# A two-layer macaron transformer in float32: the ternary weights' rounding cut into sixteenths, halves of the next group normalized a tile later, and the last 64 hidden features multiplied in rounded float32

## The chip, the cores and the metric

The kernel runs on one core of one Trainium2 chip. The metric is the device time of one execution in microseconds; lower is better. The time before is 2608.78 us, the median of 3 runs (2608.46 to 2609.09). Five engines work beside each other, each with its own queue in program order: TensorE (PE; its weight loads are PEld), VectorE (DVE), ScalarE (ACT), GpSimd (POOL) and SyncE (SP), whose queue issues nearly all DMAs here.

## The reference, cut to what matters

The input is 8 x 1024 tokens of 256 features, float32. Six blocks follow each other; each works on a layer norm of `x` and adds to `x`.

```python
x = x + 0.5 * L0_ffn(layernorm(x), w_gate, w_up, w_down)   # fp4 stage 1
x = x + L0_attn(layernorm(x), ...)                         # decaying linear attention
x = x + 0.5 * L0_ffn(layernorm(x), w_gate, w_up, w_down)   # fp4 stage 2, the same weights
x = x + 0.5 * L1_ffn(layernorm(x), W1, b1, W2, b2)         # ternary weights, gelu
x = x + L1_attn(layernorm(x), ...)                         # linear attention with memories
x = x + 0.5 * L1_ffn(layernorm(x), W1, b1, W2, b2)

def L0_ffn(x, w_gate, w_up, w_down):        # 256 -> 704 -> 256
    h = silu(fp4(x) @ fp4(w_gate).T) * (fp4(x) @ fp4(w_up).T)
    return fp4(h) @ fp4(w_down).T           # fp4: blocks of 16 share a scale max|.|/6,
                                            # each value goes to the nearest of 0, .5, 1, 1.5, 2, 3, 4, 6
def ternary(w):                             # W1 and W2, 256 x 1024 each
    return clip(round(w / mean(abs(w))), -1, 1)
```

## The kernel before, in words

The 8192 tokens are 64 tiles of 128 (`i`, `NT` = 64), four tiles to a group (`g`, `NG` = 16). `x` stays in SBUF throughout. The diff touches the two fp4 stages (`ffn_fp4`, L745), the preparation that the first of them carries along, and the decaying attention at one place.

**One tile of an fp4 stage** is one turn of the loop at L994. PE makes gate and up products in halves of 352 columns (`products`, L831: `pg` and `pu`, 2 contraction parts each; the trace has two records for each float32 matmul). ACT makes silu of `pg` (L846), DVE multiplies by `pu` (L848): that is `h`, 704 wide. Then `h` is rounded to the fp4 grid: DVE makes the blocks' scales (`scale`, L783 to L787), POOL multiplies `h` by their reciprocals (L791), ACT makes magnitudes (L795), and DVE rounds in two steps (L858, the second into `gd`, bfloat16, 768 wide with 64 columns of zeros). `gd` is turned by a DMA transpose (`gt`, L884). The scales are turned on PE (L863), sent to DRAM and read back, spread over partitions, as `ht` (L871 and L876). Two tiles later POOL multiplies `ht` by `gt` (`scaled_turn`, L905, at L899). One turn after that, `down` (L925) makes six products of 128 features each (the last has 64 features and 64 zeros) into `po`, and DVE adds `po` to `x` (L941).

**Halves of the next group.** The layer norm of group `t` is prepared during the tiles before it, in halves of two tiles: ACT normalizes (L317 and L325) at turns 4t-7 and 4t-5, DVE makes scales (L783 to L787 on `xn`) at the even turns 4t-6 and 4t-4, and DVE rounds (L858 on `xn`) at the odd turns 4t-5 and 4t-3. POOL multiplies `xn` (L791) after the scales, and `xt` by the turned grid (L899, `xt<-gtx,xt`) two turns after the rounding. The statistics for it (L235, L236, L248 to L264) are shares of work that `PLANS` (L346) lays over the turns, each group with a due turn; `ln.advance` does the shares of a turn.

**Order.** `pin` (L190) ties each instruction to the one emitted before it on the same engine, so that in these stages each queue runs in the order of the text. On DVE a turn is: L848 of the first half, the two L858 of the tile before, L848 of the second half, the scales of `h`, the work on `xn`, a share of statistics, L941, and last what `prepared(i)` (L946) brings.

**`prepared`** runs in the first fp4 stage only. At turns 7 and 27 it loads W1 and W2 (raw_w, 2048 columns per partition), and at every fourth turn after that it does one of four steps (`prep_ternary`, L674): the sum of magnitudes (L683), the total, and two roundings of 1024 columns each, three DVE instructions long (L699, L700, L703). At turn 44 it calls `prep_memory` (L719), which makes constants for the second attention, mostly on POOL.

**The end of a stage.** The last two tiles are turned by PE transposes (`turn`, L911) and not by DMA.

Of the kernel before, what the change touches and what calls it, by code (L numbers as in the profile page):

```python
# [18 lines left out]
P = 128  # L19
# [20 lines left out]
def macaron_kernel(  # L40
# [227 lines left out]
    def statistics(sizes, dues):  # L268
# [78 lines left out]
        "start": ((2, 1, 1, 2, 4, 4, 2), [max(0, G * (g - 2) + 1) for g in range(NG)]),  # L347
        "fp4": ((2, 1, 1, 2, 4, 4, 2), [max(0, G * (g - 2) + 1) for g in range(NG)]),
# [95 lines left out]
    wd = w_f0.tile([P, NC, D], F32, name="wd")  # L444
    nc.gpsimd.memset(wd[DCH[-1][1] :, NC - 1, :], 0.0)
# [190 lines left out]
    def prep_down_turn(ps, tag):  # L636
        for i, (k0, kn) in enumerate(DCH):
            pt = ps.tile([P, D], F32, tag=tag, name="ptd")
            for c in range(2):
                pin(  # L640
                    nc.tensor.transpose(
                        pt[:kn, c * P : (c + 1) * P], wd_n[:, c, k0 : k0 + kn], ident
                    )
                )
            pin(nc.scalar.copy(wd[:kn, i, :], pt[:kn, :]))
# [28 lines left out]
    def prep_ternary(w, raw_w, prep, ps, tag):  # L674

        n0 = w.shape[1]
        n = n0 * w.shape[2]
        ab = prep.tile([P, 1], F32, tag="t_ab", name="t_ab")
        rc = prep.tile([P, 1], F32, tag="t_rc", name="t_rc")

        def sums():
            pin(
                nc.vector.tensor_reduce(  # L683
                    ab, raw_w.rearrange("p k n -> p (k n)"), AX.X, ALU.add,
                    apply_absolute_value=True,
                )
            )

        def total():
            pa = ps.tile([P, 1], F32, tag=tag, name="pa")  # L690
            pin(nc.tensor.matmul(pa, lhsT=ones, rhs=ab, start=True, stop=True))
            pin(nc.vector.tensor_scalar(rc, pa, 1.0 / (P * n), 1e-8, ALU.mult, ALU.max))
            pin(nc.vector.reciprocal(rc, rc))

        def rounded(q):
            part = slice(q * n0 // 2, (q + 1) * n0 // 2)
            wf = raw_w[:, part, :].rearrange("p k n -> p (k n)")
            lo = prep.tile([P, n // 2], F32, tag="t_lo", name="t_lo")
            pin(nc.vector.tensor_scalar(wf, wf, rc, None, ALU.mult))  # L699
            pin(nc.vector.tensor_scalar(lo, wf, -0.5, None, ALU.is_lt))  # L700

            pin(
                nc.vector.scalar_tensor_tensor(  # L703
                    w[:, part, :].rearrange("p k n -> p (k n)"), wf, 0.5, lo,
                    ALU.is_gt, ALU.subtract,
                )
            )

        return sums, total, lambda: rounded(0), lambda: rounded(1)
# [35 lines left out]
    def ffn_fp4(prepare, after):  # L745
        with ExitStack() as st:
# [13 lines left out]
            nc.gpsimd.memset(gd[:, NI:], 0.0)  # L760
# [18 lines left out]
            def scale(v, pool, at, mul=nc.gpsimd, sc=None):  # L779
                vb = v.rearrange("p (b k) -> p b k", k=16)  # L780
                _, nb, _ = vb.shape
                am, sp = qp[:, at : at + nb], qp[:, at + nb : at + 2 * nb]
                pin(nc.vector.tensor_reduce(am, vb, AX.X, ALU.max, apply_absolute_value=True))  # L783
                pin(nc.vector.tensor_scalar(sp, am, -1.0 / 6.0, -1e-12, ALU.mult, ALU.min))
                rs = pool.tile([P, nb], F32, tag="q_rs", name="q_rs")
                pin(nc.vector.tensor_scalar(rs, sp, -FP4_TIE, None, ALU.mult))
                pin(nc.vector.reciprocal(rs, rs))  # L787
                if sc is None:
                    sc = pool.tile([P, nb], F32, tag="q_sc", name="q_sc")
                copies.append(lambda: pin(nc.scalar.copy(sc, sp)))  # L790
                pin(mul.tensor_tensor(vb, vb, rs[:, :, None].to_broadcast([P, nb, 16]), ALU.mult))  # L791
                return sc
# [111 lines left out]

            def scaled_turn(i):  # L905
                hs.pop(i)
                ht = spreading.pop(i)
                multiplied(ht, turning.pop(i))
                hts[i] = (ht, P)

            def turn(i):  # L911
                h, _ = hs.pop(i)
                ht = hp.tile([P, NC, P], F32, tag="ht", name="ht", bufs=HT_BUFS)
                for c0, c1 in ((0, 4), (4, 5), (5, 6)):
                    kn = DCH[c0][1]
                    pa = ps_t.tile([P, 4, P], F32, tag="pt", name="pt")
                    for c in range(c0, c1):
                        k0 = DCH[c][0]
                        pin(
                            nc.tensor.transpose(pa[:kn, c - c0, :], h[:, k0 : k0 + kn], ident)  # L920
                        )
                    pin(nc.scalar.copy(ht[:kn, c0:c1, :], pa[:kn, : c1 - c0, :]))
                hts[i] = (ht, DCH[-1][1])

            def down(i, ps=ps_o, tag="po"):  # L925
                g, j = divmod(i, G)
                ht, tail = hts.pop(i)
                po = ps.tile([P, D], F32, tag=tag, name="po")
                for c in range(NC):
                    kn = tail if c == NC - 1 else P  # L930
                    pin(
                        nc.tensor.matmul(  # L932
                            po,
                            lhsT=ht[:kn, c, :],
                            rhs=wd[:kn, c, :],
                            start=(c == 0),
                            stop=(c == NC - 1),
# [8 lines left out]
            def prepared(i):  # L946
# [10 lines left out]
                for k, i0 in enumerate((7, 27)):  # L957
# [8 lines left out]
                    if i0 < i <= i0 + 16 and i % G == i0 % G:  # L966
                        raw_w[1][(i - i0) // G - 1]()
                    if i == i0 + 16:
                        raw_w_stack.close()
                if i == 44:  # L970
                    with behind():
                        prep_memory()
# [14 lines left out]

            xn = None
# [5 lines left out]
            for i in range(NT + 3):  # L994
                g, j = divmod(i, G)
                h = hp.tile([P, NI], F32, tag="h", name="h") if i < NT else None

                to = (i + 7) // G
                to_do = to < NG and i > 0
                half = 0 if j in (1, 2, 3) else 1  # L1000
# [3 lines left out]
                pts = None  # L1004
                for q in range(2):
# [18 lines left out]
                    if 0 < i < NT and q == 0:  # L1024
                        magnitudes(hs[i - 1][0], qp[:, 0:NI])
                        if by_dma(i - 1):
                            round_grid(hs[i - 1][0], qp[:, 0:NI], gd[:, :NI])
                    if i == NT - 1:
# [15 lines left out]
                for to_, half_ in list(xgrids):  # L1044
                    gx, at = xgrids[to_, half_]
                    if at == i - 1:
                        gt = lnp.tile([P, G, P], BF16, tag="gtx", name="gtx", bufs=1)
                        pin(nc.sync.dma_start_transpose(out=gt, in_=gx))
                        xgrids[to_, half_] = (gt, at)
# [7 lines left out]
                if to_do and j % 2 == 1:  # L1057
                    if j == 1:
                        to_n, tiles = to, (0, 1)
                        if xn is None:  # L1060
                            xn = xn_pool.tile([P, G, D], F32, tag="xn", name="xn")
                    else:
                        to_n, tiles = (i + 5) // G, (2, 3)
                    if to_n < NG:
                        for n in tiles:
                            ln.normalize(xn, to_n, n, pin)
                if by_dma(i - 3):
                    scaled_turn(i - 3)
                if NT - 2 <= i - 2 < NT:
                    turn(i - 2)  # L1070
                for key in list(xgrids):
                    gt, at = xgrids[key]
                    if at == i - 2:
                        xgrids.pop(key)
                        to_m, half_m = key
                        multiplied(xts[to_m][:, G * half_m : G * half_m + G, :], gt)
                if i < NT:
                    own = scales[i % 2] if by_dma(i) else None
                    if own is not None:
                        scale(h, hp, NI, sc=own[:, : NI // 16])  # L1080
# [4 lines left out]
                    if j % 2 == 0 and i > 1:  # L1085
                        to_s, half_s = ((i + 6) // G, 0) if j == 2 else ((i + 4) // G, 1)
                        if 1 < to_s < NG:
                            scale(
                                x_part(half_s), lnp, NI + 88,
                                sc=own[:, NC * 8 : NC * 8 + 2 * D // 16],  # L1090
                            )
                            xhalf[i] = (to_s, half_s)
                    if j % 2 == 1 and i > 1:
                        to_r, half_r = ((i + 5) // G, 0) if j == 3 else ((i + 3) // G, 1)
                        if 1 < to_r < NG:
                            v = x_part(half_r)
                            mg = ps_t.tile([P, 2 * D], F32, tag="pt", name="mgx")
                            magnitudes(v, mg)
                            gx = v.bitcast(BF16)[:, 0 : 2 * D]
                            round_grid(v, mg, gx)  # L1100
                            xgrids[to_r, half_r] = (gx, i)
# [10 lines left out]
                if prepare and i == DOWN:  # L1112
                    prep_down_turn(ps_t, "pt")
# [240 lines left out]
    def attn_decay(after):  # L1354
        with ExitStack() as st:
# [101 lines left out]
            for i in range(n + 3):  # L1457
# [56 lines left out]
                if i < n:  # L1514
# [5 lines left out]
                    ln.advance(i)  # L1520
                if n - 16 <= i < n - 4:
# [563 lines left out]
```

## Time and profile before

| what | us |
|---|---|
| median of 3 runs | 2608.78 |
| the profiled execution | 2604.35 |
| its span, first to last instruction | 2602.6 |
| PE busy in the span | 2504.2 (96%) |
| DVE busy | 2107.9 (81%) |
| ACT busy | 1235.8 (47%) |
| POOL busy | 902.6 (35%) |
| first gate product of tile 8 and of tile 63, fp4 stage 1 | 114.6 and 537.5 |
| first gate product of tile 18 and of tile 63, fp4 stage 2 | 1144.4 and 1479.1 |

A row of the timeline gives the start in us, the duration in us, the engine, the line, the operation, the tiles written and read with their sizes, the count, and in brackets the idle time before it with what ended it. Instructions of one kind that follow each other are merged in one row. In DVE rows, durations of neighbours overlap by about 0.1 us, so costs are read from start to start.

### The profile page before, as it was taken

The numbers are of one execution on the slowest core, as the hardware profiler recorded it, in microseconds if no ns is written. First come the engines' busy times: TensorE is split into PE (matmuls) and PEld (weight loads), VectorE is DVE, ScalarE is ACT, GpSimd is POOL, SyncE is SP. The second block draws the span as 40 slices with busy tenths as digits, with TensorE's granted clock in tenths as the row PEclk, the third lists the DMA queues.
The fourth block names the chain that finished last, engine by engine and source line by source line (L and its number), as shares of the span: only waits on it lengthen the run. The fifth ranks groups of instructions, "written<-read, shape, count | busy, mean of one in ns | idle before, by whom it ended". The sixth has DMA issues, their size and how long they took to land.

```text
span 2602.6 us, 52695 instructions
## 1 busy us (share of the span) xinstructions
PE 2504.2 (96%) x20426; PEld 1864.2 (72%) x20426; DVE 2107.9 (81%) x5040; ACT 1235.8 (47%) x2785; POOL 902.6 (35%) x895
## 2 busy tenths in 40 slices
PE   4899999999999998999999999999999999999999
PEld 2566776766666665677777789995677767678998
DVE  7899999858777678998889789657888888879864
ACT  5344444433433333444444366665555555437664
POOL 4555555521100102555555400004555555540000
PEclk9899999999999999999999999999999999999999
DMA  7455565510000001556555300000000000000001
GB/s 218 99 111 120 119 114 112 110 32 2 2 2 2 2 2 29 113 117 116 115 114 118 81 1 1 1 1 1 2 2 2 2 2 2 2 2 25 33 33 42
DMA packets 197883, 130.32 MB, mean 50 GB/s; under 512 B 137824, under 2 KB 173696, under 8 KB 197632
## 3 DMA queue, kind: packets, MB, share of 16 engines
q1 hardware_dynamic: 196688, 125.75, 22.3%
q8 instruction: 161, 2.64, 0.4%
q0 software_dynamic: 240, 0.54, 0.1%
q14 instruction: 90, 0.74, 0.1%
q10 hardware_dynamic: 704, 0.66, 0.1%
HBM read 78.67 MB, written 16.52 MB: 37 GB/s over the span
## 4 chain that ended last, share of the span: by engine, by line
PE 80%; DVE 11%; ACT 3%; DMA 3%; issue 2%; POOL 1%; SPq 1%; DVEq 0%; POOLq 0%; ACTq 0%
PE po L932 10%; PE po L1207 9%; PE pg L835 9%; PE ph L1180 9%; PE pu L835 8%; PE sc L1250 5%; PE py L1334 5%; PE pq L1348 4%; PE pkv L1348 4%; PE pk L1348 4%; PE po L1348 4%; PE py L1316 2%; PE pmo L1765 2%; DVE at L1259 1%; DMA gtx<-xn 1%
## 5 line engine op out<-in xcount | busy, mean ns | idle before, releaser
L835 PE MATMUL pg<-wgu,xt 128*128 128x352 f32 x1024 | 350.0, 465 | 13.4 <-ACT sg L846 13.1
L932 PE MATMUL po<-wd,ht 128*128 128x256 f32 x1536 | 356.0, 382 | 2.3 <-DVE x L941 1.8
L835 PE MATMUL pu<-wgu,xt 128*128 128x352 f32 x1024 | 348.9, 464 | 2.1 <-DVE h L848 1.9
L932 PEld LDWEIGHTS po<-wd,ht 128*128 128x128 f32 x1536 | 291.7, 191 | 66.0 <-issue 4.1
L791 POOL TENSOR_TENSOR h<-h,q_rs 128x704 f32<-128x704 f32 (+1 forms) x128 | 176.3, 1378 | 419.9 <-DVE q_rs L787 419.9
L846 ACT ACTIVATE sg<-pg 128x352 f32<-128x352 f32 x256 | 117.8, 460 | 399.3 <-PE pg L835 394.0
L835 PEld LDWEIGHTS pg<-wgu,xt 128*128 128x128 f32 x1024 | 194.9, 192 | 108.5 <-ACT sg L846 21.1
L835 PEld LDWEIGHTS pu<-wgu,xt 128*128 128x128 f32 x1024 | 187.1, 193 | 103.3 <-issue 14.7
L1207 PE MATMUL po<-w,hl 128*128 128x256 f32 x1024 | 243.9, 280 | 1.4 <-DVE hl L1191 1.2
L1207 PE MATMUL po<-w,hh 128*128 128x256 f32 x1024 | 243.4, 280 | 0.0
L1881 POOL TENSOR_TENSOR mo<-mo 128x256 f32<-128x256 f32 x192 | 164.3, 856 | 195.0 <-DVE mo L1778 186.5
L899 POOL TENSOR_TENSOR ht<-gt,ht 128x768 f32<-128x768 bf16 x124 | 206.4, 1664 | 0.0
L1180 PE MATMUL ph<-xh,w 128*128 128x512 f32 x512 | 204.4, 401 | 1.4 <-ACT hf L1188 0.6
L1180 PE MATMUL ph<-xl,w 128*128 128x512 f32 x512 | 202.2, 396 | 0.0
L1191 DVE TENSOR_TENSOR hl<-hf,hh 128x512 fp32r<-128x512 f32 x256 | 168.2, 683 | 39.6 <-ACT hh L1189 36.1
L1207 PEld LDWEIGHTS po<-w,hl 128*128 128x128 f32 x1024 | 192.1, 188 | 4.5 <-DVE hl L1191 2.5
L1207 PEld LDWEIGHTS po<-w,hh 128*128 128x128 f32 x1024 | 192.0, 188 | 2.6 <-DVE x L1215 0.3
L848 DVE TENSOR_TENSOR h<-sg,pu 128x352 f32<-128x352 f32 x256 | 131.6, 514 | 60.0 <-PE pu L835 53.1
L1188 ACT ACTIVATE hf<-ph,b1c 128x512 f32<-128x512 f32 x256 | 168.3, 696 | 18.5 <-PE ph L1180 16.1
L1259 DVE TENSOR_TENSOR at<-sc,dec 128x512 f32<-128x512 f32 x256 | 158.5, 681 | 16.6 <-PE sc L1250 16.5
L1259 DVE TENSOR_TENSOR at<-sc,tri 128x512 f32<-128x512 f32 x256 | 164.6, 678 | 0.4 <-PE sc L1250 0.4
L1189 ACT CAST hh<-hf 128x512 fp32r<-128x512 f32 x256 | 149.2, 628 | 17.0 <-PE po L1207 15.2
(276 smaller groups left out, 5304.0 us busy)
## 6 DMA issues: line engine op xcount, KB each, us to landing
ht<-sd SPq DMA_DIRECT2D x124, 384.0 KB
xt<-sd SPq DMA_DIRECT2D x56, 256.0 KB
sd<-sct SPq DMA_DIRECT2D x124, 64.0 KB
x<-in_x SPq DMA_DIRECT2D x15, 512.0 KB
out<-x SPq DMA_DIRECT2D x15, 512.0 KB
raw_w<-in_w_t SPq DMA_DIRECT2D x2, 1024.0 KB
gt<-gd SPq DMA_TRANSPOSE x124
gtx<-xn SPq DMA_TRANSPOSE x56
```

Source lines behind the costliest of these rows:

```text
L791: pin(mul.tensor_tensor(vb, vb, rs[:, :, None].to_broadcast([P, nb, 16]), ALU.mult))
L835: nc.tensor.matmul(ps, lhsT=xts[g][:, 2 * j + k, :], rhs=wgu[:, k, (2 * q + of_up) * NHALF : (2 * q + of_up + 1) * NHALF], start=(k == 0), ...
L899: nc.gpsimd.tensor_tensor(wide.rearrange("p c t -> p (c t)"), grid.rearrange("p c t -> p (c t)"), wide.rearrange("p c t -> p (c t)"), ALU. ...
L932: nc.tensor.matmul(po, lhsT=ht[:kn, c, :], rhs=wd[:kn, c, :], start=(c == 0), stop=(c == NC - 1),)
L1180: nc.tensor.matmul(ph, lhsT=w1[:, k, f * P : (f + 1) * P], rhs=xt[:, k, :], start=(k == 0 and xt is xh), stop=(k == 1 and xt is xl),)
L1188: nc.scalar.activation(hf, ph, AF.Gelu, bias=b1c[:, f : f + 1])
L1189: nc.scalar.copy(hh[:, f, :], hf)
L1191: nc.vector.tensor_tensor(hl[:, f, :], hf, hh[:, f, :].bitcast(F32), ALU.subtract)
L1207: nc.tensor.matmul(po, lhsT=ht[:, f, j * P : (j + 1) * P], rhs=w2[:, f, :], start=(f == 0 and ht is hh), stop=(f == NF - 1 and ht is hl),)
L1259: nc.vector.tensor_tensor(at, sc.rearrange("p m (e t) -> p (m e) t", e=2), weight, ALU.mult)
L1348: nc.tensor.matmul(dst, lhsT=lhsT, rhs=rhs, start=n == 0, stop=n == len(parts) - 1)
L1881: summed = nc.gpsimd.tensor_tensor(mo[:, :, :, 0, :], mo[:, :, :, 0, :], mo[:, :, :, m, :], ALU.add)
```

## The change

- `prep_ternary` is cut finer: 4 sums of 512 columns, the total, and 16 roundings of 128 columns, one piece at each turn from 9 to 29 (W1) and from 36 to 56 (W2).
- `prep_memory` goes from turn 44 of fp4 stage 1 to turn 24 of the decaying attention.
- ACT normalizes a half at the turn of its scales (4t-6 and 4t-4), one turn later than before; the statistics' due turns are one later, and before fp4 stage 2 three groups are ready instead of two.
- The last 64 features of `down`: the 64 columns are written twice into `gd` (a POOL copy), their scales twice into the scale tile (an ACT copy of 4 columns), so that `ht` has them on partitions 0 to 63 and again on 64 to 127. `ws` holds the last weights rounded to fp32r on the first 64 partitions and what the rounding left on the other 64. ACT makes `hh`, the last part of `ht` rounded to fp32r (at the turn of `scaled_turn`), and POOL makes `hl = ht - hh` a turn later. Two fp32r products, `hh` by `ws` and `hl` by `ws`, take the place of one float32 product.
- `scaled_turn` and the multiplication of `xt` go to the top of the turn, behind the remainder of the tile before; no other POOL instruction was between these places.

```diff
-        "start": ((2, 1, 1, 2, 4, 4, 2), [max(0, G * (g - 2) + 1) for g in range(NG)]),
-        "fp4": ((2, 1, 1, 2, 4, 4, 2), [max(0, G * (g - 2) + 1) for g in range(NG)]),
+        "start": (
+            (2, 1, 1, 2, 4, 4, 2), [0 if g < 2 else G * (g - 2) + 2 for g in range(NG)]
+        ),
+        "fp4": ((3, 1, 2, 4, 4, 2), [0 if g < 3 else G * (g - 2) + 2 for g in range(NG)]),
...
-    wd = w_f0.tile([P, NC, D], F32, name="wd")
+    wd = w_f0.tile([P, NC - 1, D], F32, name="wd")
+    ws = w_f0.tile([P, D], F32R, name="ws")
...
+                wh = spare[:, 1, :].bitcast(F32R)
+                pin(nc.scalar.copy(wh, pt))
+                pin(nc.scalar.copy(ws[:NK], pt[:NK]))
                 pin(
+                    nc.vector.tensor_tensor(
+                        ws[NK:], pt[NK:], wh[NK:].bitcast(F32), ALU.subtract
+                    )
+                )
...
+        n_sums, n_parts = 4, 16
...
         def rounded(q):
-            part = slice(q * n0 // 2, (q + 1) * n0 // 2)
-            wf = raw_w[:, part, :].rearrange("p k n -> p (k n)")
+            part = slice(q * n // n_parts, (q + 1) * n // n_parts)
+            wf = rv[:, part]
...
             pin(nc.vector.tensor_scalar(wf, wf, rc, None, ALU.mult))
             pin(nc.vector.tensor_scalar(lo, wf, -0.5, None, ALU.is_lt))
...
+            def high_part(ht):
+                hh = hp.tile([P, P], F32R, tag="hh", name="hh", bufs=3 if prepare else 2)
+                pin(nc.scalar.copy(hh, ht[:, NC - 1, :]))
+                return hh
+
+            def remainder(ht, hh):
+                hl = hp.tile([P, P], F32R, tag="hl", name="hl", bufs=3 if prepare else 2)
+                pin(
+                    nc.gpsimd.tensor_tensor(
+                        hl, ht[:, NC - 1, :], hh.bitcast(F32), ALU.subtract
+                    )
+                )
+                return hl
...
             def down(i, ps=ps_o, tag="po"):
...
+                factors = [(ht[:, c, :], wd[:, c, :]) for c in range(NC - 1)]
+                factors += [(hh, ws), (hl, ws)]
...
-                for k, i0 in enumerate((7, 27)):
+                for k, i0 in enumerate((7, 34)):
...
-                    if i0 < i <= i0 + 16 and i % G == i0 % G:
-                        raw_w[1][(i - i0) // G - 1]()
+                    if i0 + 1 < i <= i0 + 1 + 21:
+                        raw_w[1][i - i0 - 2]()
...
-                if i == 44:
-                    with behind():
-                        prep_memory()
...
+            for t in range(2, NG):
+                for half in range(2):
+                    at = G * t - 6 + 2 * half
+                    norms[at] = x_scales[at] = x_rounds[at + 1] = (t, half)
...
+                if by_dma(i - 4) and i <= NT:
+                    hts[i - 4] += (remainder(*hts[i - 4]),)
+                if by_dma(i - 3):
+                    scaled_turn(i - 3)
...
                             round_grid(hs[i - 1][0], qp[:, 0:NI], gd[:, :NI])
+                            pin(nc.gpsimd.tensor_copy(gd[:, NI:], gd[:, NI - NK : NI]))
...
                 if by_dma(i - 3):
-                    scaled_turn(i - 3)
+                    hts[i - 3] += (high_part(hts[i - 3][0]),)
...
+                if i == 24:
+                    with behind():
+                        prep_memory()
```

The last two tiles of a stage get the doubled columns by two POOL copies in front of their transposes, which are grouped in threes instead of 4, 1 and 1.

## The prediction

> **What bounds the kernel now.** I began with the busy tenths of the page and went on to the timeline of the fp4 stages, since the change lies there.
>
> ```profile
> PE   4899999999999998999999999999999999999999
> DVE  7899999858777678998889789657888888879864
> PEclk9899999999999999999999999999999999999999
> ```
>
> PE is full nearly everywhere at the full clock, but in the fp4 stages (slices 2 to 8 and 16 to 22) DVE stands at eight or nine tenths too. Two engines are near their limit there. The timeline of PE in stage 1 gives the period of a tile:
>
> ```profile
> 307.03 2.75 PE L932 MATMUL po<-wd,ht 128*128 128x256 f32 x12
> 309.62 1.35 PE L835 MATMUL pg<-wgu,xt 128*128 128x352 f32 x4
> ...
> 314.46 2.75 PE L932 MATMUL po<-wd,ht 128*128 128x256 f32 x12
> ```
>
> One down starts 7.43 us after the other, with PE never idle between: a tile costs PE 7.43. Its 12 records of down take 309.62 - 307.03 = 2.59, so 0.216 each, and a float32 product is two records, 0.432. In stage 2, tiles 18 to 63 come every 7.44 (45 in 334.8 us): PE alone bounds them. In stage 1, from tile 8's first gate product to tile 63's, 55 tiles take 422.9 us, 14 more than 55 x 7.43.
>
> DVE's own cycle I read from an even turn (scales of `xn`), where it ran almost without a gap:
>
> ```profile
> 383.90 0.89 DVE L783 TENSOR_REDUCE qp<-h 128x44 f32<-128x704 f32 x1
> ...
> 387.06 0.37 DVE L235 BATCH_NORM_STATS2 ln_s<-x 128x6 f32<-128x256 f32 x1
> ...
> 387.56 0.39 DVE L941 SCALAR_TENSOR_TENSOR x<-po,x 128x256 f32<-128x256 f32 x1
> 387.87 0.51 DVE L848 TENSOR_TENSOR h<-sg,pu 128x352 f32<-128x352 f32 x1
> ...
> 390.80 0.90 DVE L783 TENSOR_REDUCE qp<-h 128x44 f32<-128x704 f32 x1
> ```
>
> From scales to scales it is 6.90; less a gap of 0.13 and the statistics (0.50) it is 6.27. The odd turn before it (rounding of `xn`), 377.19 to 383.90, is 6.71, less 0.52 of waiting for a magnitude: 6.19. So DVE has about 1.2 us to spare beside PE's 7.43, and each share of statistics takes 0.5 of it.
>
> **The rounded product.** It removes one float32 product, 0.432, and adds two of fp32r. The nearest row is the ternary down, the same shapes: 64 of them (L1207) take 7.54 in the chain of the run (from 1571.65 on), 0.118 each. So 0.432 - 2 x 0.118 = 0.196 less PE per tile: 7.44 becomes 7.24. From both sides: nothing, if an fp32r product behind a float32 one costs as much as a record of that (0.216), and 0.196 at most. I take 0.196, because shapes and weight loads (188 against 191 ns a load) are alike. What it adds elsewhere is off the path: `hl` on POOL about 0.42 (L666, 128x128, 0.46, three in 1.29), the copy into `gd` and the copy of scales 0.2 each (an ACT copy of 44 columns is 0.19), `hh` on ACT 0.26 (as L869). ACT is 40% busy; POOL, 55%, has queues but ends them before DVE's next reciprocals. On odd turns the `gd` copy stands behind POOL's `ht` and `xt`, so the transpose is issued some 2 us later; `ht` is wanted 11 us after its issue at 316.94 and the last of it lands at 322.0. That cover is 6 us wide. The later normalization (2.0 on ACT) lies beside the scales of `h` (1.75 on DVE); at most 0.3 shows, inside DVE's spare time.
>
> In stage 2, tiles 18 to 62 gain 45 x 0.196 = 8.8. Tiles 6 to 17 carry 2.5 to 3 shares: DVE 6.23 + 2.5 x 0.5 = 7.5, over PE's new 7.24, so they keep their time; I give the first 18 tiles 0.5 in all. **Stage 2: -9.3.**
>
> **The weights' pieces.** This step decides. A rounding of 1024 columns came four times in all of stage 1; now one of 128 columns comes at 32 turns. Its three instructions work in SBUF alone, and beside a busy POOL they do not run freely. The timelines of DVE and of POOL around one of the old roundings:
>
> ```profile
> 211.88 1.01 DVE L699 TENSOR_SCALAR raw_w<-raw_w,t_rc 128x1024 f32<-128x1024 f32 x1
> 212.92 2.03 DVE L700 TENSOR_SCALAR t_lo<-raw_w 128x1024 f32<-128x1024 f32 x1
> 214.98 1.22 DVE L703 SCALAR_TENSOR_TENSOR w<-raw_w,t_lo 128x1024 fp32r<-128x1024 f32 x1
> ```
>
> ```profile
> 211.05 1.29 POOL L666 TENSOR_TENSOR dec<-dec,tri 128x128 f32<-128x128 f32 x3
> 212.29 2.11 POOL L899 TENSOR_TENSOR ht<-gt,ht 128x768 f32<-128x768 bf16 x1
> ```
>
> L700 takes 0.69 in its three other places; here 2.03, and it ends 0.55 after POOL's L899 does. L899, else 1.66, takes 2.11, since it waited for L699. They take turns, one instruction each. The second attention shows the same with tiny instructions that have two inputs in SBUF:
>
> ```profile
> 1848.91 0.29 DVE L263 TENSOR_TENSOR ln_h<-ln_h,ln_r 128x12 f32<-128x12 f32 x1
> 1849.23 0.65 DVE L264 SCALAR_TENSOR_TENSOR ln_r<-ln_h,ln_r 128x12 f32<-128x12 f32 x1
> ```
>
> L264 is 0.17 when POOL rests; here POOL's L1968 row (`y<-y,mo`, 1849.13 to 1849.86) holds it. Such waits don't shrink with the columns.
>
> The Trainium skill (SBUF — State Buffer, "SBUF: two separate sides") says it as a rule that speaks against this change: VectorE and GpSimd share a pair of SBUF ports as an exclusive lock, held for a whole instruction, against VectorE instructions in a two-port mode or with two SBUF inputs. It adds that a whole instruction is waited for, not a share of the bandwidth. By that rule each of the three can wait for one whole POOL instruction, which is what the sum below finds from the rows; without the rule the free price below would stand.
>
> Free, a piece costs 0.22 + 0.24 + 0.28, about 0.75 (128 columns on the slope of L700 and L703 from the 16 columns of L255, 0.16). Now the turn by hand, time 0 at the reciprocals' end (385.75). **Even:** POOL has L791 until 1.5, `xn` until 2.6, then `hl`, then `ht`. DVE ends the scales of `xn` at 1.3 and L941 at 1.6 (2.1 with a share). L699 waits for `xn` and ends at 2.7; `hl` goes, to 3.1; L700 ends at 3.2; `ht` goes, to 4.8; L703 ends at 4.9. The next L848 starts at 4.8 instead of 1.6 or 2.1, so the turn is 6.27 + 3.2 = 9.5, with a share or without. **Odd:** the piece starts at 1.6 to 2.1, L699 waits for `hl` or `ht`, L700 for `ht`; it ends at 4.1 to 4.3: 6.19 + 2.4 = 8.6. Mean 9.05. Bounds: 0.75 a piece below (turn 7.6 with its 1.25 shares), and above, `xt` (1.17) in line before L703 as well, 10.6 on even turns.
>
> Behind the piece on DVE stand L848 and L858; PE waits for L848 (`pu`), so PE becomes idle 1.8 us a tile.
>
> Stage 1 from tile 8, in us: tile 8, 7.6; 9 to 13 (3 to 2.5 shares, a sum of 0.65: L683's 2.28 for 2048 columns shows no wait beside L899) 5 x 8.3 = 41.5; 14 to 17 (2.5 shares) 4 x 9.2 = 36.8; 18 to 29, 12 x 9.05 = 108.6; 30 to 40, 11 x 7.24 = 79.6; 41 to 56, 16 x 9.05 = 144.8; 57 to 62, 43.4. Sum 462.3 against 422.9. **Stage 1: +39.4**, what the bursts and `prep_memory` cost before (the 14) already gone.
>
> **The rest.** `prep_memory` in the attention: its one DVE wait was 1.92, for a DMA; DVE is 70% busy there, so 0 to 2, I take 1. The turned weights with the split, 0 to 2, 1. The last two tiles of each stage get two POOL copies and the split, 0 to 2 a stage, 1 each. **+4.**
>
> Sum: -9.3 + 39.4 + 4 = +34. The span goes from 2602.6 to 2636.7, the profiled execution from 2604.35 to 2638.4; the median shown lies 4.4 above that execution, so 2608.8 + 34 = **2643**.
>
> **Rivals.** (a) *The pieces run free*, because POOL's row is through before they come: POOL is idle 45% of the time. Against it: L941 ends 1.6 to 2.1 after the reciprocals and POOL's row runs from 0.1 to 4.6. Then 28 turns at 7.6 and 4 at 8.25 make stage 1 417.9, -5; in all -10: 2598. This one is faster. It decides from 8.0 us a turn: there the gain on PE is just eaten. (b) *L703 does not wait*, as no run shows that instruction beside POOL: even 7.95, odd 8.55, +10: 2618. (c) *`xt` stands in line too*: 16 even turns with 1.2 more, 2662. (d) *The fp32r products bring nothing*: 2643 + 9 = 2652.
>
> **Chances.** Main 0.45, a 0.26, b 0.12, c 0.11, d 0.06. What a measurement can tell here is 0.2%, 5 us. Case a spreads some 6 us around 2598, so 0.22 of it is faster and 0.04 the same; of b 0.02 is the same. Faster 0.22, same 0.06, slower 0.72. The range takes in a's middle and c: 2596 to 2664; below it half of a (0.13) and above it a part of c are left out.
>
> **What will show it.** Right: tiles 18 to 62 of stage 2 at 7.24; L1207-like records of 0.118 at the end of down; in stage 1, L699, L700 and L703 with means near 0.9 instead of 0.25, and turns near 9 in 14 to 29 and 41 to 56; POOL's `ht` not delayed more than 0.3. Wrong: means of the three below 0.4 (a), only L703 short (b), down unchanged in length (d), or stalls on `hh`, `hl` or `gt`, which I have at nothing.

## The result and the profile after

The changed kernel takes **2683.5 us**, the median of 4 runs (2679.22 to 2685.9); the kernel before, beside it, 2608.62. The ratio is 1.0286 [1.0268, 1.0304]: 75 us slower. The forecast was 2643, from 2596 to 2664: the sign is right, and the time lies 20 us above the range.

The profiled execution took 2685.9 us, its span is 2684.0. These are the busy tenths of the page after:

```profile
PE   4888898889999999999999889999999999999999
DVE  7799989976777677988778669865888888889864
PEclk9899999999999999999999999999999999999999
```

The granted clock is as before. PE has lost its nines in slices 2 to 4 and 6 to 8 (counted from 0), where stage 1 has its pieces, and in slices 22 and 23 too. That was not forecast: stage 2 has no pieces. Where the 81.4 us of the two spans came from, in us, read as in the front table from the first gate product of a tile:

| stretch | before | after | forecast change | change |
|---|---|---|---|---|
| stage 1, tile 8 to 63 | 423.0 | 472.6 | +39.4 | +49.6 |
| stage 2, tile 0 to 18 | 138.4 | 134.4 | -0.5 | -4.0 |
| stage 2, tile 18 to 63 | 334.8 | 366.6 | -8.8 | +31.8 |
| all else | 1706.4 | 1710.4 | +4 | +4.0 |

**The rounded product is as forecast.** PE after, where nothing stalls it (timeline of PE, stage 2):

```profile
1341.12 2.32 PE L978 MATMUL po<-wd,ht 128*128 128x256 f32 x10
1343.09 0.47 PE L978 MATMUL po<-ws,hh 128*128 128x256 f32 x1
1343.40 0.28 PE L978 MATMUL po<-ws,hl 128*128 128x256 f32 x1
1343.51 1.34 PE L865 MATMUL pg<-wgu,xt 128*128 128x352 f32 x4
...
1348.36 2.32 PE L978 MATMUL po<-wd,ht 128*128 128x256 f32 x10
```

From down to down it is 1348.36 - 1341.12 = 7.24, the forecast to the hundredth. But only every other turn of stage 2 is so short: from tile 18 to 58, turns have means of 7.29 and 8.77 in alternation, and near the end turns 59 and 60 take 13.35 and 10.29.

**The pieces wait as forecast.** The groups of DVE, with the mean in ns behind the comma:

```profile
L728 DVE SCALAR_TENSOR_TENSOR w<-raw_w,t_lo 128x128 fp32r<-128x128 f32 x32 | 29.4, 920 | 1.1
L724 DVE TENSOR_SCALAR raw_w<-raw_w,t_rc 128x128 f32<-128x128 f32 x32 | 27.1, 846 | 0.0
L725 DVE TENSOR_SCALAR t_lo<-raw_w 128x128 f32<-128x128 f32 x32 | 16.3, 509 | 1.1
```

They have shortest instances of 270 (L724), 226 (L725) and 291 (L728). One turn shows the alternation, first on DVE, then on POOL:

```profile
416.66 1.09 DVE L724 TENSOR_SCALAR raw_w<-raw_w,t_rc 128x128 f32<-128x128 f32 x1
417.78 0.38 DVE L725 TENSOR_SCALAR t_lo<-raw_w 128x128 f32<-128x128 f32 x1
418.20 1.64 DVE L728 SCALAR_TENSOR_TENSOR w<-raw_w,t_lo 128x128 fp32r<-128x128 f32 x1
```

```profile
416.61 1.06 POOL L821 TENSOR_TENSOR xn<-xn,q_rs 128x512 f32<-128x512 f32 x1
417.63 0.45 POOL L943 TENSOR_TENSOR hl<-ht,hh 128x128 fp32r<-128x128 f32 x1
418.04 1.65 POOL L929 TENSOR_TENSOR ht<-gt,ht 128x768 f32<-128x768 bf16 x1
```

Each of the three ends 0.1 after one POOL instruction: L724 after `xn`, L725 after `hl`, L728 after `ht`. Turns 14 to 29 and 41 to 56 have means of 8.98 and 8.96; forecast 9.05.

**What was not forecast** is in stage 2, in the chain of waits after (start, us, what it consists of):

```profile
1341.92 6.83 DMA sd<-sct
...
1348.80 0.60 SPq L906
...
1349.45 4.75 DMA gtx<-xn
...
1354.37 0.14 POOL xt L929
...
1355.44 0.24 POOL gd L1078
1355.68 1.35 POOL h L821
...
1357.06 0.77 ACT qp L825
...
1357.85 0.90 DVE h L888
1358.75 0.02 issue
1358.77 0.90 DVE gd L888
```

There is no PE in it for 17 us. The reader is to see who stands behind whom:

- SP's queue: the issue of `ht` (L906) waits for the scales `sd` to land in DRAM, and the transpose `gtx` for the next group's half stands behind it, so it goes out at 1349.45 only.
- POOL's queue: `xt` (L929) waits for `gtx`. Behind `xt` stands the new copy into `gd`, 0.24 long (L1078), and behind that the multiplication of `h` (L821). DVE had rounded the copy's columns by 1350.27; the copy runs at 1355.44.
- From `h` on: ACT's magnitudes (L825), DVE's rounding (L888), and the scales behind it; at 1363.42 PE has waited 1.13 for ACT's copy of the scales.
- SP's queue again: the transpose `gt` waits for the copy. Then `gt`, `ht`, `xt` and the next `sd` go out at 1355.71, 1357.05, 1357.70 and 1358.38, within 2.7 us.

The ring is closed by the last of these. The turn before shows its issues on SP:

```profile
1340.59 0.60 SPq L906 DMA_DIRECT2D ht<-sd  x1
1341.28 0.58 SPq L906 DMA_DIRECT2D xt<-sd  x1
1341.92 0.57 SPq L901 DMA_DIRECT2D sd<-sct  x1
...
1348.80 0.60 SPq L906 DMA_DIRECT2D ht<-sd  x1
1349.45 1.20 SPq L1106 DMA_TRANSPOSE gtx<-xn  x1
```

The 64 KB of `sd`, issued just behind 384 and 256 KB, take 6.83 us. So `ht` and `gtx` are late again, `xt` is late, the copy is late: a `gtx` at 1332.93, at 1349.45 and at 1365.51, 16.1 to 16.5 for two turns that PE could do in 14.5. POOL's waits after, tiles 18 to 63 of stage 2 (us in total, times, longest):

```profile
POOL xt L929 <- DMA gtx<-xn: 57.7, 16, 6.0
```

### The profile page after: what moved, and what is told of

The parts are those of the page before. It is cut to its first block, busy times and chain, and to the rows that moved or that the text cites. A ratio compares the mean times of both kernels' runs of the same rounds, so it can differ in the third digit from the quotient of the medians.

```text
span 2684.0 us, 53288 instructions
## 1 busy us (share of the span) xinstructions
PE 2505.5 (93%) x20426; PEld 1850.4 (69%) x20426; DVE 2153.9 (80%) x5121; ACT 1269.1 (47%) x3034; POOL 981.6 (37%) x1154
## 4 chain that ended last, share of the span: by engine, by line
PE 59%; DVE 16%; DMA 6%; issue 5%; ACT 3%; POOL 3%; SPq 0%; POOLq 0%; DVEq 0%; ACTq 0%
PE po L1246 9%; PE ph L1219 8%; PE sc L1289 5%; PE py L1373 4%; PE pq L1387 4%; PE pkv L1387 4%; PE pk L1387 4%; PE po L1387 4%; DMA gtx<-xn 3%; PE po L978 3%; PE pu L865 2%; PE pg L865 2%; DVE qp L809 2%; PE py L1355 2%; DMA sd<-sct 2%
## 5 line engine op out<-in xcount | busy, mean ns | idle before, releaser
L978 PE MATMUL po<-wd,ht 128*128 128x256 f32 x1280 | 307.4, 389 | 15.0 <-DVE x L983 14.5
L978 PEld LDWEIGHTS po<-wd,ht 128*128 128x128 f32 x1280 | 247.1, 196 | 77.2 <-POOL hl L943 15.5
L865 PEld LDWEIGHTS pg<-wgu,xt 128*128 128x128 f32 x1024 | 185.9, 192 | 127.1 <-ACT sg L876 48.0
L821 POOL TENSOR_TENSOR h<-h,q_rs 128x704 f32<-128x704 f32 (+1 forms) x128 | 176.2, 1377 | 213.3 <-DVE q_rs L813 208.2
L929 POOL TENSOR_TENSOR ht<-gt,ht 128x768 f32<-128x768 bf16 x124 | 205.2, 1655 | 0.0
L1230 DVE TENSOR_TENSOR hl<-hf,hh 128x512 fp32r<-128x512 f32 x256 | 168.8, 686 | 39.4 <-ACT hh L1228 35.9
L1298 DVE TENSOR_TENSOR at<-sc,dec 128x512 f32<-128x512 f32 x256 | 158.6, 683 | 16.5 <-PE sc L1289 16.4
L825 ACT ACTIVATE qp<-h 128x704 f32<-128x704 f32 x126 | 96.0, 762 | 140.3 <-POOL h L821 133.6
```

What stands on the lines that cost most here:

```text
L865: nc.tensor.matmul(ps, lhsT=xts[g][:, 2 * j + k, :], rhs=wgu[:, k, (2 * q + of_up) * NHALF : (2 * q + of_up + 1) * NHALF], start=(k == 0), ...
L929: nc.gpsimd.tensor_tensor(wide.rearrange("p c t -> p (c t)"), grid.rearrange("p c t -> p (c t)"), wide.rearrange("p c t -> p (c t)"), ALU. ...
L978: nc.tensor.matmul(po, lhsT=left, rhs=right, start=(n == 0), stop=(n == NC))
L1230: nc.vector.tensor_tensor(hl[:, f, :], hf, hh[:, f, :].bitcast(F32), ALU.subtract)
L1298: nc.vector.tensor_tensor(at, sc.rearrange("p m (e t) -> p (m e) t", e=2), weight, ALU.mult)
```

## The experiments

Two theories stood against each other for what the forecast missed, 40.5 us by the medians and 47.3 by the spans (2684.0 against 2636.7). **The ring:** the copy into `gd` behind `xt` on POOL, as above. **The rival:** the pieces cost more than their own wait, since POOL's instructions wait for them too and all queues run later. Beside that it was open what the pieces, the order and the product are worth each. Line numbers shift a little from kernel to kernel; the operations and tiles name the same work.

**e1: the copy ahead of `xt`.** After, with the multiplication of `xt` moved behind the copy:

```diff
                     scaled_turn(i - 3)
-                for key in list(xgrids):
-                    gt, at = xgrids[key]
...
                     turn(i - 2)
+                for key in list(xgrids):
+                    gt, at = xgrids[key]
...
```

> The changed kernel with one move: GpSimd multiplies xt behind the copy into gd, and not in front of it. Theory of the loop (the copy stands behind xt, xt waits for the transpose of the half's grid, which SP issues behind ht, which waits for the scales, which land behind the xt transfer that the copy let start): in fp4 stage 2 the 45 turns from tile 18 fall from 366.6 us to 326 to 330, all at 7.24, and in stage 1 the turns 30 to 40 from 7.98 to 7.3. Theory of the waits at the pieces (three VectorE instructions, each behind one of GpSimd's): turns 14 to 29 and 41 to 56 stay at 8.5 to 9.1; total about 2632. Rival, that the loop alone is behind all of it: these turns fall to 7.6 as well, total about 2586.

Measured: 2638.94 us, 1.0118 [1.0101, 1.0135]. Stage 2 from tile 18 falls from 366.6 to 326.9, turns of 7.24 and 7.27. Stage 1 from tile 8 falls by 6.2 only, 472.6 to 466.4. POOL's waits in e1 from 1150 to 1515:

```profile
POOL xt L929 <- DMA gtx<-xn: 9.8, 12, 3.2
```

SP's waits for the landing of `sd` fall with it, first in after (1190.8 to 1557.4), then in e1 (1150 to 1515):

```profile
SPq L906 <- DMA sd<-sct: 68.9, 21, 4.8
```

```profile
SPq L906 <- DMA sd<-sct: 12.3, 15, 2.0
```

The ring is shown: one POOL instruction of 1.16 us, moved past one of 0.24, brings 45 us back. In stage 1 it had cost little, because the pieces hold the turns near 9 us anyway, and the ring alone needs 8.0 to 8.3 (16.1 to 16.5 for two).

**e7: the ring cut at another link.** After, with SP issuing `gtx` ahead of `sd`, `gt` and `ht`:

```diff
+                for to_, half_ in list(xgrids):
+                    gx, at = xgrids[to_, half_]
...
                 if pts is not None:
                     spread(i - 1, pts)
...
                     ln.advance(i - 1, 1)
-                for to_, half_ in list(xgrids):
-                    gx, at = xgrids[to_, half_]
...
```

> The changed kernel with one other move: SP issues the transpose of the half's grid (gtx) ahead of the tile's scales, gd and ht, while xt stays in front of the copy on GpSimd. Theory of the loop: it is cut at another link, so stage 2 comes to 326 to 332 for the 45 turns and the turns 30 to 40 of stage 1 to about 7.5, total 2632 to 2642. Rival, that the copy simply comes too late behind xt, loop or not: stage 2 stays above 350.

Measured: 2644.07 us, 1.0145 [1.0131, 1.016]; stage 2 from tile 18 takes 332.2. POOL does not wait for `gtx` once between 1150 and 1515, while SP's waits there are still:

```profile
SPq L906 <- DMA sd<-sct: 50.4, 25, 3.6
```

Of the 5.3 us over e1's 326.9, nearly all lie in one turn (59, with 12.54 against 7.38). So the late landing of `sd` costs nearly nothing by itself. It costs when `gtx`, then `xt`, then the copy hang on it.

**e5: the copy alone, in the kernel before.** It copies columns that meet zeros, so the computation stays as it was.

```diff
-            nc.gpsimd.memset(gd[:, NI:], 0.0)
...
                             round_grid(hs[i - 1][0], qp[:, 0:NI], gd[:, :NI])
+                            pin(nc.gpsimd.tensor_copy(gd[:, NI:], gd[:, 2 * NI - NC * P : NI]))
```

> The kernel before, with the copy of 64 columns into gd on GpSimd as its only edit (the copied columns meet scales of zero, as the zeros did). Theory of the loop: the copy alone closes it, so the 45 turns of stage 2 go from 334.8 us to about 361 to 366 (some 16.1 per two turns), stage 1 gains 10 to 25 us of delay as well, total 2640 to 2660. Rival, that the loop needs the rest of the change (the remainder in GpSimd's row, the later normalization): stage 2 at 335 to 340, total below 2620.

Measured: 2675.97 us, 1.0268 [1.0254, 1.0283], 69 more than before and more than I expected: 35.2 in stage 1 from tile 8, 8.4 in the first 18 turns of stage 2 and 24.7 in the others. In that text the copy stands in front of `ht` and `xt`, and its ring has other links (POOL's and SP's waits, 1190 to 1550):

```profile
POOL gd L1027 <- DVE gd L857: 129.1, 42, 4.5
```

```profile
SPq L883 <- POOL ht L898: 71.2, 37, 2.2
```

POOL's copy waits until DVE has rounded, `ht` stands behind it, and the next `gt` waits for `ht`. This run does not show the ring of after; it shows that 0.24 us of POOL per tile, badly placed, cost 69 us by themselves, with the old pieces and the old down.

**e2: the old roundings of the weights**, four of 1024 columns, in the kernel after.

```diff
-        n_sums, n_parts = 4, 16
...
+        n0 = w.shape[1]
+        n = n0 * w.shape[2]
...
-            part = slice(q * n // n_parts, (q + 1) * n // n_parts)
...
+            part = slice(q * n0 // 2, (q + 1) * n0 // 2)
...
-                for k, i0 in enumerate((7, 34)):
+                for k, i0 in enumerate((7, 27)):
```

> The changed kernel with the weights' preparation of before (one sum, two roundings of 1024 columns, every fourth turn, loads at 7 and 27). If the pieces cost by themselves beside the loop: turns 14 to 29 and 41 to 56 of stage 1 fall from 9.0 to the 8.1 that stage 2 shows, total about 2655. If the loop alone is behind it: those turns stay near 9, total 2675 to 2685. Stage 2 stays at 366 in either.

Measured: 2661.8 us, 1.0201 [1.0186, 1.0217]. Stage 2 is as in after (365.2). Stage 1 falls by 23.1 to 449.5, not to e3's 415.0: without the pieces the ring shows there too, with 34.5. Pieces and ring cover each other in part, and their prices do not add.

**e3: e1 and e2 together.**

> Both edits of the two other kernels together. If the two causes are all there is: stage 2 at 7.24 a turn and stage 1 near 415 us from tile 8 to 63, total about 2592, faster than before by the 0.196 us a tile of the rounded product. If something else of the change costs too (the later normalization, the memories in the attention, the high parts): above 2609.

Measured: **2587.65 us, 0.9918 [0.9903, 0.9933]**, faster than both kernels by more than the spread of the runs. This is the order on POOL (timeline, stage 2):

```profile
1287.26 1.65 POOL L924 TENSOR_TENSOR ht<-gt,ht 128x768 f32<-128x768 bf16 x1
1289.02 0.24 POOL L1067 COPY gd<-gd 128x64 bf16<-128x64 bf16 x1
1289.75 1.16 POOL L924 TENSOR_TENSOR xt<-gtx,xt 128x512 f32<-128x512 bf16 x1 [0.50 <-DMA gtx<-xn]
```

`xt` still waits for its transpose, 0.50, but nothing that is urgent stands behind it. Against e1, the old pieces give 51.4 us in stage 1 (466.4 to 415.0) and nothing in stage 2 (326.9 and 327.4): the rival, that the pieces delay other stretches, falls.

**e4: the pieces alone**, in the kernel before (`prep_ternary` and its turns as in the diff, nothing else).

> The kernel before with the changed preparation of the ternary weights alone (4 sums, 16 roundings of 128 columns, a turn each). Theory of the waits: without the remainder in GpSimd's row an even piece ends about 0.4 earlier, so turns 14 to 29 and 41 to 56 go from 7.7 to about 8.7, total about 2640, and the means of the three instructions lie near 0.6 to 0.9 us instead of 0.25. Rival, that small pieces fit into VectorE's spare time: these turns at 7.6, total 2605 to 2610, means near 0.3.

Measured: 2644.21 us, 1.0135 [1.012, 1.015]; stage 1 from tile 8 takes 461.2, 38.2 more than before. With the old order of the text L702 and L703 wait (1008 and 659 ns), the third instruction hardly (L706, 334): which instruction waits depends on what POOL is doing, and the sum of the three less so (2001 ns here, 2275 in after).

**e9: the pieces by way of PSUM.** e1, with the product of the first instruction in a PSUM tile, so that no instruction of a piece has two operands in SBUF or moves from SBUF to SBUF alone.

```diff
-            pin(nc.vector.tensor_scalar(wf, wf, rc, None, ALU.mult))
-            pin(nc.vector.tensor_scalar(lo, wf, -0.5, None, ALU.is_lt))
+            tp = ps.tile([P, n // n_parts], F32, tag=tag, name="tp")
+            pin(nc.vector.tensor_scalar(tp, wf, rc, None, ALU.mult))
+            pin(nc.vector.tensor_scalar(lo, tp, -0.5, None, ALU.is_lt))
...
-                    wv[:, part], wf, 0.5, lo, ALU.is_gt, ALU.subtract
+                    wv[:, part], tp, 0.5, lo, ALU.is_gt, ALU.subtract
```

> The run with the pieces in PSUM once more (xt behind the copy, each piece's first instruction writes to PSUM), but into a tile of its own and not into qp: there ScalarE's copies of the scales, which read qp, waited for the piece (83.0 us in 32 waits), a wait that the edit itself made. Theory of the waits: the three stay at about 0.34, 0.29 and 0.29 us, nothing waits for them, the turns 14 to 29 and 41 to 56 fall from 8.9 to 7.4 to 7.8, total 2583 to 2600. Rival, that the number of small instructions costs by itself: these turns above 8.3, total above 2618.

Measured: 2597.23 us, 0.996 [0.9948, 0.9973]. The groups of DVE:

```profile
L725 DVE TENSOR_SCALAR tp<-raw_w,t_rc 128x128 f32<-128x128 f32 x32 | 11.0, 345 | 0.0
L726 DVE TENSOR_SCALAR t_lo<-tp 128x128 f32<-128x128 f32 x32 | 9.3, 292 | 1.1
L729 DVE SCALAR_TENSOR_TENSOR w<-tp,t_lo 128x128 fp32r<-128x128 f32 x32 | 9.3, 291 | 1.1
```

In e1 these were 869, 509 and 887. The same instructions at the same places beside the same POOL work lose 1337 ns a piece, once one operand lies in PSUM, and no instance of the three is longer than 347, 293 and 292 ns; stage 1 falls from 466.4 to 424.3. That the pieces wait for POOL where they work in SBUF alone is shown.

The Trainium skill (SBUF — State Buffer, "SBUF: two separate sides") lets only VectorE instructions in a two-port mode or with two SBUF inputs wait for GpSimd; the three means of e9 agree with that.

**e6: the same, into a part of `qp`**, the PSUM tile of the magnitudes, in place of a tile of its own.

> The changed kernel with xt behind the copy, and with the 16 pieces kept, but each piece's first instruction writes to a spare part of the PSUM tile qp, so that none of the three works from SBUF into SBUF alone nor has two inputs in SBUF. Theory of the waits: the turns 14 to 29 and 41 to 56 fall from 8.9 to 7.4 to 7.7, the means of the three instructions to 0.2 to 0.35 us, total 2583 to 2595. Rival, that it is the number of small instructions that costs: these turns stay above 8.4 and the total above 2620.

Measured: 2624.24 us, 1.0068 [1.0054, 1.0081], 29 above the upper end. The means are as in e9 (344, 291, 291), so the pieces run free, but ACT's waits have a new row:

```profile
ACT sc L817 <- DVE w L729: 83.0, 32, 4.1
```

ACT's copy of the scales reads `qp` too, and now waits for the last instruction of the piece, 32 times in 32 pieces. A tile shared for convenience made a wait that cost some 27 us (e6 less e9).

**e10: the pieces earlier on DVE**, ahead of the scales of `h` and no longer at the turn's end, otherwise e1.

```diff
-                    if i0 + 1 < i <= i0 + 1 + 21:
-                        raw_w[1][i - i0 - 2]()
                     if i == i0 + 22:
...
+                for i0 in (7, 34) if prepare else ():
+                    if i0 + 1 < i <= i0 + 1 + 21:
+                        raw_w[1][i - i0 - 2]()
                 if i < NT:
```

> The changed kernel with xt behind the copy, and the pieces as they are, but emitted ahead of the scales of h instead of at the end of the turn: the same instructions on the same data, at a place where GpSimd has ended its row and waits for the scales. Theory of the waits: on even turns they meet nothing, on odd turns xt at the most; means of the three 0.25 to 0.55 us, the turns 14 to 29 and 41 to 56 at 7.5 to 8.0, total 2588 to 2608. Rival, that it is their number: the turns stay at 8.9 and the total at 2639. A third case: the place is on VectorE's longest chain (h, scales, GpSimd, magnitudes), and each piece delays it by its own 0.8: turns near 8.0 to 8.3, total 2608 to 2620.

Measured: 2606.08 us, 0.9996 [0.9986, 1.0005]. Of the three only the first still waits (734, 228 and 319 ns). Stage 1 takes 433.3: of the 51.4 us between e1 and e3 there, 33.1 are gone without any change in the instructions, by their place alone; 18.3 remain.

**e8: the old order of halves**, in e3 (old `PLANS`, normalization a turn earlier).

```diff
-                    norms[at] = x_scales[at] = x_rounds[at + 1] = (t, half)
+                    norms[at - 1] = x_scales[at] = x_rounds[at + 1] = (t, half)
```

> The kernel of the third run (xt behind the copy, the old weights' preparation) with the normalization a turn earlier and the due turns of the statistics as before. If these two parts of the change are worth what the first 18 turns of stage 2 show (132.4 against 138.4 us, of which 18 x 0.196 = 3.5 is the product): about 2.5 us more in stage 2, 0 to 5 in stage 1, total 2590 to 2597. If they are worth nothing: 2587 to 2589.

Measured: 2609.27 us, 1.0007 [0.9998, 1.0016]: 22 more than e3 and outside both expectations. ACT's and DVE's waits in e8 between 1150 and 1470:

```profile
ACT xn L317 <- DMA gtx<-xn: 35.6, 20, 4.3
```

```profile
DVE xn L881 <- ACT mgx L818: 14.1, 17, 1.8
```

A turn earlier, the normalization on ACT waits for the `gtx` that still reads its buffer, and what ACT has behind it is late for DVE. In e3 this wait is 3.3 us in the same stretch, in before 10.8. In stage 1 (113 to 540) it is 51.5 in e8, 3.0 in e3 and 36.1 in before.

**e11: the order alone**, in the kernel before.

> The kernel before with the new order of halves and the later normalization alone: down keeps its one float32 product of 0.432 us, the pieces are the old ones. Theory (the order is worth something only once TensorE is no longer the bound of stage 2): tiles 18 to 63 of stage 2 stay at 334.8 us, 7.44 each; its first 18 turns, which the ScalarE normalization of 138.4 us held up, come to some 135; total 2600 to 2609. Rival (the order is worth its 21 us by itself, whatever TensorE does): total about 2588.

Measured: 2600.66 us, 0.9971 [0.9961, 0.998]. Tiles 18 to 63 of stage 2 stay at 335.1; the first 18 fall from 138.4 to 131.6, and stage 1 by 1.5. So the order is worth 8 us in the kernel before and 22 in e3. The rival (21 us by itself) falls. Why it is more in e3 is not shown. ACT's wait for `gtx` that the order takes away is larger there: by the two stretches above it is 87.1 in e8 and 6.3 in e3, but 46.9 in before and 4.9 in e11. And e8 has not only the shorter turn of PE, but also the new work on ACT and POOL.

**e12: the memories back in stage 1**, at turn 44, in e3.

> The fastest version so far (xt multiplied behind the copy, old pieces), with the preparation of the memories back at turn 44 of stage 1. Theory (what was taken out of stage 1 and put into the attention costs about as much in the one place as in the other): 2586 to 2590. Rival (its DMA and its VectorE work were in the way in stage 1, and the attention hides it): 2590 to 2593, with the turns about 44 longer by 2 to 4 in sum.

Measured: 2592.87 us, 0.9943 [0.9928, 0.9957]. The span is 3.6 longer than e3's, and the tiles from 46 and 47 take 9.46 and 7.43 where e3 has 7.24 twice: 2.4 of it, inside the rival's 2 to 4. The other 1.2 is spread over single turns, which differ by up to 1 us either way (turn 26 of stage 1 is 1.08 longer, turn 59 of stage 2 is 0.59 shorter), and the intervals of e3 and e12 overlap.

## Why the prediction was wrong, step by step

- **The rounded product:** right. 7.24 a tile as forecast, wherever nothing stalls. Tiles 18 to 63 in e3 take 327.4 against 334.8, 7.4 less where 8.8 was forecast. Rival (d) is out.
- **The weights' pieces:** right in mechanism, and as a sum in size. Stage 1 was to get +39.4; the pieces alone (e4) give +38.2, and e1, which has the pieces, the product and the order without the ring, +43.4. The three means of 846, 509 and 920 stand near the 0.9 given as the sign for it, the middle one lower. Rivals (a) and (b) are out for this kernel; in e4 the third instruction is nearly free, as (b) has it, and the time is not (b)'s, because the first two wait longer. That the sum agrees so well is in part luck. In e1 an even piece takes 2.65 us from its first start to its last end and an odd one 2.01, where the sum added 3.2 and 2.4, and the 32 turns of the pieces take 284.7 us where it had 290.2. Against that, the turns behind the pieces, 30 to 40 and 57 to 62, were put at PE's 7.24 and take 83.8 and 48.4 in place of 79.6 and 43.4: the first of them are still 9.31 and 8.83 long.
- **The step that failed:** "On odd turns the `gd` copy stands behind POOL's `ht` and `xt`, so the transpose is issued some 2 us later; `ht` is wanted 11 us after its issue [...] That cover is 6 us wide." I had the order right and took `ht` and `xt` at their durations. The 2 us hold only while `xt` finds its transposed grid there. It has to wait for a DMA, and the copy inherits this wait: 5.2 us late in the turn shown. And the cover of 6 us was read from one transpose and one landing, with `sd` issued into a queue that had time. In after the late transpose also pushes `ht`, `xt` and the next `sd` together, and `sd` takes 6.83. The delay so feeds itself. It was priced at nothing and costs 48 us by the spans of after and e1 (2684.0 - 2636.1): 6.2 in stage 1 and 41.7 in stage 2. My last line named "stalls on `hh`, `hl` or `gt`, which I have at nothing" as what would make me wrong; this is it.
- **What hid behind the copy:** the copy is followed on POOL by `h`, which ACT, DVE and PE need in the same turn. I counted who waits for the copy (the transpose) and not who stands behind it.
- **Rival (c)** had DVE's piece wait for `xt` as well on even turns. In the even turn shown the piece takes 3.2 us and ends with `ht`, as in the sum; `xt` starts 3.2 later, at 422.99. Its 2662 lies nearer to the result, but by a mechanism that was not the one.
- **The order of halves:** "at most 0.3 shows" and 0.5 us for the first 18 turns were too little. They fall by 6.8 with the order alone, and in e3 the order saves 22 in all (against e8). I had looked for what the later normalization would cost and not for what it no longer waits for. This error is on the side of a gain and made the sum with e1 (2638.94 against 2643) look better than its terms: stage 2 gained 13.9 in e1, not 9.3, and stage 1 lost 43.4, not 39.4.
- **The rest:** +4 forecast, +4.0 measured, as a sum; of its parts only the memories have a run. Their +1 in the attention does not show: all else takes 1711.5 in e3 and 1712.1 in e12, which has them in stage 1. What they cost in stage 1, 2.7 (417.7 in e12 against 415.0), is part of the 14 that the sum for stage 1 had taken off.

## What to carry to other kernels

A short instruction put into a queue that runs in order can cost not its duration but the wait of what stands in front of it (here 0.24 us a tile and 48 us in all), and it passes that wait on to all that stands behind; so look for the nearest instruction ahead of it that waits for a DMA. Where a late issue makes transfers go out together, follow the smallest of them to its reader: if that reader's queue leads back to the late issue, the delay is renewed in each turn, and spare time read from one turn says nothing. Placed with care (e3) the same product and order make this kernel 0.8% faster; the weights' pieces were in no run better than the four old roundings.

## What the runs showed of the hardware

A small transfer that was issued right behind large ones landed with them: `sd` (64 KB) took 6.83 us behind `ht` and `xt` (384 and 256 KB) in after. Its semaphore, which counts a transfer's parts as they land, shows this in two halves: eight parts of `sd` landed 1.8 to 2.0 us after the issue (1343.74 to 1343.91), the other eight at 1348.29 to 1348.75, beside and behind the last of `xt` (1347.83 to 1348.52). In e3 the turn of two tiles has `ht`, `xt` and the next `sd` at 1290.62, 1291.31 and 1295.65, so that `sd` is issued 4.3 us after `xt`; `ht`, which waits for it, goes out 3.1 us after its issue (timeline of SP, one turn of two earlier):

```profile
1281.17 0.57 SPq L896 DMA_DIRECT2D sd<-sct  x1
1282.04 1.24 SPq L909 DMA_TRANSPOSE gt<-gd  x1
1284.29 0.60 SPq L901 DMA_DIRECT2D ht<-sd  x1
```

Where float32 and fp32r products follow each other, starts of single records mislead: the first fp32r product starts 0.31 ahead of the second, nearly three times 0.118, but the ten float32 records in front take 1.97 from start to start, where ten of 0.216 would be 2.16. So only the whole down is compared here, 1341.12 to 1343.51: 2.39 where it was 2.59.
